# A hand-written order for the first seven slots of an attention and expert block

## The chip, the cores and the metric

The kernel runs on one core of a Trainium2 chip. Time is the device time of one execution in microseconds (us). The median of 3 runs before the change is 843.74 us (842.83 to 845.68). The core has five engines that run side by side, each taking its own instructions strictly in the order of the program: TensorE (PE in the profile, with PEld for its weight loads), VectorE (DVE), ScalarE (ACT), GpSimd (POOL) and SyncE (SP), which here only issues transfers. They wait for each other with semaphores.

## The reference, cut to what matters

Eight sequences of 256 tokens with 256 features go through an attention layer with a layer norm before and after it, and then through a layer of eight experts and a shared expert. All is float32. Only the beginning of the attention is touched by the change.

```python
x = x + _layernorm(_L0_attn_ref(_layernorm(x), w_qkv, w_o, qn_g, qn_b, kn_g, kn_b))
x = x + _layernorm(_L0_ffn_ref(_layernorm(x), ...))
...
qkv = jnp.einsum('bsh,oh->bso', x, w_qkv)          # 16 heads of q, 4 of k, 4 of v, 128 wide
q = _layernorm(q, qn_g, qn_b)                      # per head, over its 128 features
k = _layernorm(k, kn_g, kn_b)
q = q * cos + _rotate_half(q) * sin                # the same for k
scores = jnp.einsum('bhqd,bhkd->bhqk', q, k) / jnp.sqrt(jnp.float32(D))   # causal
weights = jax.nn.softmax(scores, axis=-1)
attn = jnp.einsum('bhqk,bhkd->bhqd', weights, v)
return jnp.einsum('bsd,od->bso', attn, w_o)
```

## The kernel before

**Tiling.** A sequence is two tiles of 128 tokens. The weights w_qkv are six groups of 512 columns: groups 0 to 3 are q's heads, 4 is k and 5 is v. A *projection* is one group times one token tile, 128 x 512 (`multiply`, L366), so a sequence has twelve, taken in the order of groups 4, 5, 0, 1, 2, 3 with both tiles of each. They are numbered j = 0 to 11.

**The work on one projection.** The mean of each head's weights is taken off the weights themselves once (`centre`, L229 to L231), so that q and k come out with mean zero. Then `square` (ACT, L384), `deviation` (DVE sum of the squares, L390), `power` (POOL, to the power -1/2, L399), `normalise` (ACT, four pieces of 128, L408), `rope_cos` (DVE, L422), `rope_sin` (POOL, two halves, L434), `rope_offset` (POOL, L447), `rope_sum` (DVE, L455) and `turn_heads` (four transposes on PE, L470, and a copy on ACT, L471). A projection of v is only copied (ACT, L381). The gains and biases of the norm are folded into tables with the cosine and sine (`tables`, L213 to L222): `cg`, `sg` and `bb` for q and for k; q's are also scaled by the root of 1/128.

**The attention** of a sequence is twelve units (four groups; tile 0 with four heads, tile 1 with twice two heads): `score` (PE), `maximum` (DVE), `exponential` (ACT), `inverse` (DVE), `weights` (POOL or ACT), transposes (PE, L544), `copy_weights` (DVE, L549), `value` (PE, L562). Then come 32 output products per sequence (L581).

**The order** is written by hand: inside `tc.manual_schedule()` each engine gets its instructions in the order of the text. A loop over slots s issues, in slot s, the stages of projection s, the normalisation and rope of projection s - 1, the sum and turning of s - 2, and the unit s - 7 of the attention with its later stages behind it; outputs begin at slot 19. A slot number is a running number over sequences: twelve slots belong to each. The next sequence's x is prepared by `begins` at places 2 to 7 of the current one (`prepare`, `prepared`, `turn_x`). Before the loop come the first x and the centring of group 4; `tables("k")` is in slot 0, `tables("q")` in slot 3, and the centrings of groups 0 to 3 are in slots 1, 3, 5 and 7, all on DVE.

**Loads.** All are issued from SP in the order of the text: x of sequence 0, w of group 4, k's gain and bias (each copied from memory to all 128 partitions), cosine and sine, q's gain and bias, w of groups 5 and 0, x of sequence 1, the other w, the other x, then wo and the expert weights.

**PSUM**[...] two each for projections (`ps_mm`), transposes (`ps_tr`) and scores (`ps_sc`), one for values (`ps_av`) and one for outputs (`ps_o`).

## Time and profile before

| | |
|---|---|
| median of 3 runs | 843.74 us |
| the profiled execution | 841.31 us |
| its span | 839.6 us |
| mean granted TensorE clock | 0.974 |
| busy PE, PEld | 751.9 us (90%), 552.4 us (66%) |
| busy DVE, ACT, POOL | 551.9 us (66%), 434.1 us (52%), 487.6 us (58%) |

The page cuts the span into 40 equal slices and gives each engine's busy share in tenths (9 is 90% or more), and the TensorE clock that was granted, in tenths of full speed. A line of instructions reads: source line, engine, operation, output<-inputs, shape. "A <- B" among the waits says that A stood idle until B was done. The chain is followed back from the last instruction, at each step to what released it. Durations of PE are those of pipelined instructions: one may be reported with 592 ns and the next begin 430 ns after it.

### The profile page before, as it was taken

Reading aid. Unit: us, or ns where it says so; the run is one execution under the profiler, and the core shown is the slowest. Engines: PE = TensorE matmul, PEld = TensorE weight load, DVE = VectorE, ACT = ScalarE, POOL = GpSimd, SP = SyncE. Lnnn points to the kernel's source line nnn. Section 1 sums busy time; section 2 is a strip of 40 time slices with the busy share of each in tenths; the row PEclk is TensorE's granted clock in tenths of the full one; section 3 lists DMA queues with packets and bytes.
Section 4 is the critical chain, followed back from the end, with each engine's and each line's share of the span. In section 5 each row is a group of like instructions: output and inputs, shape, how many; then the busy total and the mean of one; then the engine's idle time right before and its main releaser. Section 6 shows DMA issues by size and latency. Waiting matters only on the chain.

```text
span 839.6 us, 11874 instructions
## 1 busy us (share of the span) xinstructions
PE 751.9 (90%) x3770; PEld 552.4 (66%) x3770; DVE 551.9 (66%) x1392; ACT 434.1 (52%) x1393; POOL 487.6 (58%) x523
## 2 busy tenths in 40 slices
PE   4478999999999999999999999998988999998881
PEld 1246667767676676767667676776767867775561
DVE  4587676778778778877877887577653443234565
ACT  1247776657556675665667566576522323332230
POOL 3387587667748766784876678487111052236653
PEclk9699999999999999999999999999999999999997
DMA  8500000000000000000000000004002022224452
GB/s 263 164 1 1 1 1 1 7 1 7 7 1 7 1 7 1 7 7 1 8 1 7 2 7 7 1 7 139 7 7 73 9 88 77 63 89 126 130 146 75
DMA packets 27485, 32.66 MB, mean 39 GB/s; under 512 B 3040, under 2 KB 23616, under 8 KB 27424
## 3 DMA queue, kind: packets, MB, share of 16 engines
q1 hardware_dynamic: 24016, 22.59, 8.6%
q0 software_dynamic: 3408, 9.31, 4.1%
q8 instruction: 31, 0.51, 0.2%
q14 instruction: 30, 0.25, 0.1%
HBM read 22.59 MB, written 9.31 MB: 38 GB/s over the span
## 4 chain that ended last, share of the span: by engine, by line
PE 57%; POOL 16%; DVE 13%; ACT 8%; issue 5%; DMA 1%; POOLq 0%; SPq 0%; DVEq 0%; ACTq 0%
PE qkv L366 11%; PE o L581 8%; PE sc L482 6%; PE av L562 5%; PE gu L968 5%; ACT qn L408 5%; POOL rstds L399 5%; POOL t L434 5%; PE py L993 4%; POOL t L447 3%; PE tp L544 3%; PE tq L470 2%; PE g L270 2%; PE u L270 2%; PE sd L286 2%
## 5 line engine op out<-in xcount | busy, mean ns | idle before, releaser
L366 PE MATMUL qkv<-w_qkv,xnT 128*128 128x512 f32 x384 | 186.0, 609 | 8.3 <-DVE w_qkv L231 3.2
L408 ACT ACTIVATE qn<-qkv,rstds 128x128 f32<-128x128 f32 x320 | 91.5, 369 | 161.1 <-POOL rstds L399 161.1
L399 POOL TENSOR_TENSOR rstds<-ves,nhalf 128x4 f32<-128x4 f32 x80 | 87.1, 1088 | 115.1 <-DVE ves L390 115.1
L434 POOL TENSOR_TENSOR t<-qn,sg_q 128x256 f32<-128x256 f32 x128 | 122.1, 973 | 50.7 <-ACT qn L408 50.7
L581 PE MATMUL o<-wo_sb,oT 128*128 128x256 f32 x512 | 128.0, 389 | 0.0
L482 PE MATMUL sc<-kT,q 128*128 128x128 f32 x768 | 110.5, 279 | 1.8 <-ACT q L471 1.8
L513 ACT ACTIVATE ex<-sc,nmx 128x128 f32<-128x128 f32 (+1 forms) x256 | 107.7, 453 | 2.7 <-DVE nmx L502 2.4
L562 PE MATMUL av<-pT,v 128*128 128x256 f32 (+1 forms) x320 | 101.4, 432 | 7.3 <-ACT oT L573 6.6
L366 PEld LDWEIGHTS qkv<-w_qkv,xnT 128*128 128x128 f32 x384 | 67.9, 197 | 60.0 <-issue 49.5
L482 PEld LDWEIGHTS sc<-kT,q 128*128 128x128 f32 x768 | 102.4, 194 | 4.9 <-ACT q L471 2.9
L581 PEld LDWEIGHTS o<-wo_sb,oT 128*128 128x128 f32 x512 | 92.4, 193 | 9.5
L455 DVE TENSOR_TENSOR t<-t,t 128x512 f32<-128x512 f32 x80 | 55.3, 692 | 51.5 <-POOL t L447 51.5
L470 PEld LDWEIGHTS tq<-ident,t 128*128 128x128 f32 x320 | 38.1, 141 | 71.1 <-issue 51.5
L447 POOL TENSOR_TENSOR t<-t,bb_q 128x512 f32<-128x512 f32 x64 | 81.8, 1277 | 3.0
L549 DVE COPY pT<-tp 128x512 f32<-128x512 f32 x96 | 65.5, 682 | 18.2 <-PE tp L544 18.1
L533 ACT ACTIVATE ex<-ex,rr 128x256 f32<-128x256 f32 x128 | 59.5, 526 | 28.6 <-DVE rr L521 28.6
L562 PEld LDWEIGHTS av<-pT,v 128*128 128x128 f32 x320 | 59.1, 192 | 19.7 <-ACT oT L573 9.7
L470 PE MATMUL tq<-ident,t 128*128 128x128 f32 x320 | 49.3, 277 | 23.4 <-DVE t L455 23.3
L941 POOL DMA_INDIRECT xb<-xf_rows,src x39 | 38.5, 988 | 52.5 <-PE xt L951 37.7
L390 DVE TENSOR_REDUCE ves<-sq 128x4 f32<-128x516 f32 x80 | 54.8, 685 | 21.4 <-ACT sq L384 21.2
L544 PEld LDWEIGHTS tp<-ident,ex 128*128 128x128 f32 x384 | 47.7, 142 | 30.2 <-ACT q L471 9.6
L502 DVE TENSOR_REDUCE nmx<-sc 128x2 f32<-128x512 f32 (+1 forms) x96 | 64.2, 668 | 4.0 <-PE sc L482 3.4
(180 smaller groups left out, 1306.5 us busy)
## 6 DMA issues: line engine op xcount, KB each, us to landing
ys<-yb SPq DMA_DIRECT2D x39, 128.0 KB
w_qkv<-in_wqkvT SPq DMA_DIRECT2D x6, 512.0 KB
x_all<-in_x SPq DMA_DIRECT2D x8, 256.0 KB
wo_sb<-in_woT SPq DMA_DIRECT2D x1, 2048.0 KB
xf_rows<-xf SPq DMA_DIRECT2D x16, 128.0 KB
out<-yo SPq DMA_DIRECT2D x16, 128.0 KB
wgu_sb<-in_wg SPq DMA_DIRECT2D x2, 704.0 KB
wgu_sb<-in_wu SPq DMA_DIRECT2D x2, 704.0 KB
```

Source lines behind the costliest of these rows:

```text
L366: nc.tensor.matmul(ps.rearrange("p h d -> p (h d)"), lhsT=seqs[b]["xnT"][t][:, c, :], rhs=w_qkv[g][:, c, :], start=(c == 0), stop=(c == KC ...
L399: nc.gpsimd.tensor_tensor(rstd, now.pop(("ve", b, j)), nhalf, ALU.pow)
L408: nc.scalar.activation(qn[:, h, :], ps[:, h, :], AF.Copy, scale=rstd[:, h : h + 1])
L434: nc.gpsimd.tensor_tensor(t2[:, :, lo : lo + HD], qn[:, :, hi : hi + HD], sg[s][:, t : t + 1, lo : lo + HD].to_broadcast([P, REP, HD]), AL ...
L447: nc.gpsimd.tensor_tensor(t2, t2, bb[s][:, t : t + 1, :].to_broadcast([P, REP, D]), ALU.add)
L470: nc.tensor.transpose(tr[:, h, :], t1[:, h, :], ident)
L482: nc.tensor.matmul(sc[:, h, k * P : (k + 1) * P], lhsT=seqs[b]["qT"][g][:, r0 + h, t * P : (t + 1) * P], rhs=seqs[b]["kT"][:, g, k * P : ( ...
L513: nc.scalar.activation(ex[:, h, :], sc[:, h, :], AF.Exp, bias=nm[:, h : h + 1], accum_out=rs[:, h : h + 1],)
L544: nc.tensor.transpose(tr[:, c, :], ex[:, h, k * P : (k + 1) * P], ident)
L549: nc.vector.tensor_copy(pT, now.pop(("tp", b, u)).rearrange("p c q -> p (c q)"))
L562: nc.tensor.matmul(now["av"][:, r0 : r0 + nh, :].rearrange("p h q -> p (h q)"), lhsT=seqs[b]["v"][:, k, g * D : (g + 1) * D], rhs=pT[:, k ...
L581: nc.tensor.matmul(now["o", b, t], lhsT=seqs[b]["oT"][h // REP, t][:, h % REP, :], rhs=wo_sb[:, h, :], start=(h == 0), stop=(h == H - 1),)
```

## The change

Nothing is changed in what is computed. The loop now begins at slot 7; what slots 0 to 6 did is written out as a list. In it:

- 24 transposes of the identity come first on PE; their result is not read.
- The first sequence's projections are taken as v tile 0, k tile 0, k tile 1, v tile 1, then q as before. Projections 0, 3, 4 and 5 write to banks of scores, values and outputs.
- The offset is added to the cosine product on DVE (`rope_offset_early`) for projections 1, 2, 4, 5 and 6, in place of POOL's `rope_offset`.
- `centre` is split: `means` finds the negative mean on DVE; group 4 is centred on DVE, and groups 0 to 3 on ACT in eight pieces each (`centre_on_act`). Those of groups 2 and 3 are in slots 7 and 9.
- Gains and biases are loaded as four rows in one partition and multiplied by a row of ones on PE, which lays them on all 128 partitions; ACT copies the product to SBUF. q's rows are scaled before that, in place of q's tables. k's tables are made on POOL and q's on DVE.
- ACT issues the loads of these rows and of cosine and sine; SP issues x of sequence 0, w of groups 4, 5, 0, then x of sequence 1 and the rest.
- x of sequence 1 is prepared in slots 7 to 10 in place of slots 2 to 7; that of the other sequences is prepared where it was.

In the diff, the renaming of `projections[j]` to `projections[b][j]` is left out.

```diff
     load_x(0)
-    w_qkv = {4: load_w(4)}
+    w_qkv = {g: load_w(g) for g in groups[:3]}
...
-    gb = {}
-    for s, ga, ba in (("k", kn_g, kn_b), ("q", qn_g, qn_b)):
-        for n, a in (("g", ga), ("b", ba)):
-            gb[s, n] = sh.tile([P, 1, D], F32, tag=f"{n}_{s}", name=f"{n}_{s}", bufs=1)
-            nc.sync.dma_start(out=gb[s, n][:, 0, :], in_=a.partition_broadcast(P))
-        if s == "k":
-            nc.sync.dma_start(out=cos_sb, in_=cos.rearrange("(t p) d -> p t d", p=P))
-            nc.sync.dma_start(out=sin_sb, in_=ssin.rearrange("(t p) d -> p t d", p=P))
+    gb_all = sh.tile([P, 4, D], F32, tag="gb", name="gb_all", bufs=1)
+    gb_row = gb_all[0:1]
+    for n, a in enumerate((kn_g, kn_b, qn_g, qn_b)):
+        nc.scalar.dma_start(out=gb_row[:, n, :], in_=a[None, :])
+    nc.scalar.dma_start(out=cos_sb, in_=cos.rearrange("(t p) d -> p t d", p=P))
+    nc.scalar.dma_start(out=sin_sb, in_=ssin.rearrange("(t p) d -> p t d", p=P))
...
+    ones_row = scratch[0:1, 2 * NT, :]
+    nc.gpsimd.memset(ones_row, 1.0)
...
-    def tables(s):
+    def tables(s, engine):
...
-        if s == "q":
-            for tab in (cg[s], sg[s], bb[s]):
-                nc.vector.tensor_scalar_mul(tab, tab, scale)
-
-    def centre(g):
+    def means(g):
         heads = w_qkv[g].rearrange("p c (h d) -> p (c h) d", d=D)
         wm = small.tile([P, KC * REP], F32, tag="wm", name=f"wm_{g}")
         nc.vector.tensor_reduce(out=wm, in_=heads, axis=AX.X, op=ALU.add)
-        nc.vector.tensor_scalar_mul(wm, wm, 1.0 / D)
+        nc.vector.tensor_scalar_mul(wm, wm, -1.0 / D)
+        return heads, wm
...
+    def centre_on_act(heads, wm):
+        for i in range(KC * REP):
+            nc.scalar.activation(
+                heads[:, i, :], heads[:, i, :], AF.Identity, bias=wm[:, i : i + 1]
+            )
...
+        projections = [[(5, 0), (4, 0), (4, 1), (5, 1)] + rest[4:]] + [rest] * (B - 1)
...
+            spare = {0: (ps_sc, "sc"), 3: (ps_sc, "sc"), 4: (ps_av, "av"), 5: (ps_o, "o")}
+            pool, tag = spare.get(b * NS + j, (ps_mm, "mm"))
+            ps = pool.tile([P, REP, D], F32, tag=tag, name=f"qkv_{b}_{j}")
...
+        def rope_offset_early(b, j):
...
+            nc.vector.tensor_add(t1, t1, bb[s][:, t : t + 1, :].to_broadcast([P, REP, D]))
...
         with tc.manual_schedule():
+            warm = ps_tr.tile([P, 4, P], F32, tag="tr", name="warm")
+            for k in range(WARM):
+                nc.tensor.transpose(warm[:, k % 4, :], ident, ident)
             for t in range(NT):
                 prepare(0, t)
+            for t in range(NT):
                 prepared(0, t)
+            found[4] = means(4)
             for t in range(NT):
                 turn_x(0, t)
+            centre(*found.pop(4))
+            multiply(0, 0)
+            nc.vector.tensor_scalar_mul(gb_row[:, 2:], gb_row[:, 2:], scale)
+            gbp = ps_o.tile([P, 4, D], F32, tag="o", name="gbp")
+            nc.tensor.matmul(
+                gbp.rearrange("p n d -> p (n d)"), lhsT=ones_row,
+                rhs=gb_row.rearrange("p n d -> p (n d)"), start=True, stop=True,
+            )
+            nc.scalar.copy(gb_all, gbp)
+            found[0] = means(0)
+            tables("k", nc.gpsimd)
+            tables("q", nc.vector)
+            centre_on_act(*found.pop(0))
+            multiply(0, 1)
+            square(0, 0)
+            square(0, 1)
+            multiply(0, 4)
             nc.vector.tensor_copy(identb, ident)
-            centre(4)
-            for s in range(B * NS + OUT + 5):
...
+            deviation(0, 1)
+            power(0, 1)
+            found[1] = means(1)
+            square(0, 4)
+            multiply(0, 2)
+            multiply(0, 5)
+            normalise(0, 1)
+            deviation(0, 4)
+            power(0, 4)
+            rope_cos(0, 1)
+            rope_offset_early(0, 1)
+            rope_sin(0, 1)
+            normalise(0, 4)
+            square(0, 2)
+            rope_cos(0, 4)
+            rope_offset_early(0, 4)
+            rope_sin(0, 4)
+            deviation(0, 2)
+            power(0, 2)
+            centre_on_act(*found.pop(1))
+            rope_sum(0, 1)
+            turn_heads(0, 1)
+            rope_sum(0, 4)
+            turn_heads(0, 4)
+            multiply(0, 3)
+            multiply(0, 6)
+            normalise(0, 2)
+            square(0, 3)
+            square(0, 5)
+            rope_cos(0, 2)
+            rope_offset_early(0, 2)
+            rope_sin(0, 2)
+            deviation(0, 5)
+            power(0, 5)
+            found[2] = means(2)
+            normalise(0, 5)
+            square(0, 6)
+            rope_sum(0, 2)
+            turn_heads(0, 2)
+            rope_cos(0, 5)
+            rope_offset_early(0, 5)
+            rope_sin(0, 5)
+            deviation(0, 6)
+            power(0, 6)
+            for s in range(FIRST, B * NS + OUT + 5):
```

## The prediction

> **What bounds the kernel now.** I read the page's slices first, then busy time by stretch, then the waits and the chain of the first 60 us, then the timeline there.
>
> ```profile
> PE   4478999999999999999999999998988999998881
> DVE  4587676778778778877877887577653443234565
> POOL 3387587667748766784876678487111052236653
> PEclk9699999999999999999999999999999999999997
> ```
>
> A slice is 21 us. PE is full from the sixth slice to near the end; in the first two it is under half busy, and the second has granted clock 0.6. The stretches, in columns PE, PEld, DVE, ACT, POOL, granted clock, DMA share, GB/s:
>
> ```profile
> 11.00:53.00 42.00, 24.32 (x55) 11.08 (x55) 25.52 (x49) 10.32 (x28) 18.79 (x19) 0.80 0.52 171
> 53.00:117.00 64.00, 55.87 (x277) 36.96 (x276) 45.26 (x80) 44.32 (x148) 46.36 (x46) 0.97 0.00 1
> 117.00:600.00 483.00, 467.21 (x2477) 345.33 (x2476) 364.69 (x880) 308.10 (x1019) 333.33 (x339) 1.00 0.03 10
> ```
>
> Slots 0 to 6 lie in 11 to 53 us and no engine is more than 61% busy there: this stage is bound by waiting. The waits of the first 60 us (us in total, times, longest) say for whom:
>
> ```profile
> POOL rstds L399 <- DVE ves L390: 21.4, 2, 11.9
> ACT qn L408 <- POOL rstds L399: 17.3, 6, 4.6
> PEld tq L470 <- DVE t L455: 14.2, 3, 8.1
> ```
>
> and the chain (start, us, what) says why:
>
> ```profile
> 26.61 1.34 DVE xn L251
> 27.96 0.33 DVE cg_q L213
> ...
> 30.50 1.14 DVE wm L229
> 31.66 0.18 DVE wm L230
> 31.87 1.23 DVE w_qkv L231
> 33.09 0.61 DVE t L455
> 33.71 0.04 issue
> 33.75 1.12 PE tq L470 x4
> 34.87 3.43 PE qkv L366 x4
> ```
>
> VectorE works strictly in order. The sum of k's second tile (L455) stands behind q's tables and a centring; PE, with nothing to do meanwhile, falls to half clock and takes 3.43 us for four matmul pieces that take 1.73 later. From 53 to 117 us (slots 7 to 18) the chain alternates between POOL and ACT's normalisation, about 5.5 us a slot: L399 1.0, L408 1.15, L434 1.92, L447 1.26. From slot 19 PE carries the chain. Everything after slot 7 follows its predecessor, so time saved before slot 7 moves the end by as much, unless slots 7 to 10 return it.
>
> **How I cost the start.** I put the new order of instructions into the four engines' queues: each starts at the later of its engine's freedom and its inputs, with spacings from rows (VectorE 128x512 tensor op 0.61, reduction 0.60, weight-mean reduction 1.13 plus 0.17; POOL power 1.0; ACT normalisation 4 x 0.29; square or copy 0.48; projection 1.73 at full clock, 3.43 at half). One thing more is needed, seen in the timeline:
>
> ```profile
> 18.61 0.69 DVE L422 TENSOR_TENSOR t<-qn,cg_k 128x512 f32<-128x512 f32 x1 [2.31 <-ACT qn L408]
> 26.55 1.26 POOL L447 TENSOR_TENSOR t<-t,bb_k 128x512 f32<-128x512 f32 x1
> 26.61 1.34 DVE L251 TENSOR_SCALAR xn<-x_all,mv_x,rstd_x 128x256 f32<-128x256 f32 x1 [1.08 <-POOL rstd_x L246]
> ```
>
> The xn scaling takes 0.41 at its fastest, and 1.34 when it starts just behind a POOL tensor op, ending 0.14 after it: whichever has begun, the other waits. Reductions and POOL's power are not caught in this (L390 keeps 0.69 beside POOL). The same walk over the old order puts the normalisation of slot 7 (projection 6) at 51.7 us and that of projection 10 at 73.7; the trace has 52.52 and 74.27. It is 0.6 to 0.8 short, which I carry over.
>
> **The new start, in order.** (1) x lands at 3.6, as before; both tiles are normalised by 6.1. (2) The mean of group 4's weights, 1.21 + 0.18, now precedes the two 0.42 copies of the turned x: 7.8. In the old order the first projection waited until 11.37 for the centring, since it was k; now it is v, which needs none. (3) That projection, 7.8 to 9.7; the product with ones, two pieces of 0.43, to 10.5; ACT's copy 0.6, to 11.15. (4) q's tables on VectorE, seven ops, 1.9 us (27.96 to 29.89 in the old chain); k's on POOL beside them. POOL's 256-element op takes 0.73 (the residual add) and its 512-element one 1.26, so 0.46 for 128: 3 x 0.66 + 4 x 0.40 as spacings, 3.6. Under the exclusion they run one after the other: 11.15 + 1.9 + 3.6 = 16.7. (5) Power of k's first tile to 17.7; normalisation to 18.8. (6) Then VectorE's run of cosine, offset, cosine, offset, 18.9 to 21.4, keeps POOL's sines out until 21.3; sines of projections 1 and 4 to 24.6; power of 2 to 25.6; its normalisation behind two head copies to 27.7; sines to 30.3; power of 5, normalisation to 32.4; sines 33.7 to 35.1; power of 6 to 36.0. Slot 7's normalisation starts at 36.1. (7) PE idles from 18.8 to 24.0. The trace's clock fell to 0.5 about 25 to 38 us, around such a gap, so I let projection 3, and what follows to 28 us, run at half: v's copy is late on ACT, with the next square behind it; 1.5 us. Slot 7 at 37.6, with 0.6 carried over 38.2, against 52.5: **14.3 us won.**
>
> **What slots 7 to 10 return.** Centring of groups 2 and 3 goes to ACT, 8 x 0.29 = 2.3 us each, ahead of the exponentials in slots 7 and 9; the next normalisation queues behind. ACT idled 1.74 and 0.94 us before those. The second sequence's x moves to slots 7 to 10: two power ops of 0.55 on POOL, two scalings and copies of 0.4 on VectorE; slot 7's offset (1.26) leaves POOL. The walk has 23.3 us from projection 6's normalisation to that of 10, against 22.0 in the old order: **1.3 to 1.5 us back.** At 0.37 per ACT piece, its reported length, slot 9 loses 1.4 more.
>
> **Edits that I cost at nothing.** The six loads moved to ACT's queue: about 0.45 us of issue each (2.7 us) in ACT's idle first 10 us; without that cover they would delay the copy of step 3. SP then has x, w4, w5, w0 in a row. With the tables beside them, 1.57 MB must land by 7.8 us for step 3: from 2.0 us at 300 GB/s 7.2 us; at the 228 of the first active microsecond 8.9, which costs 1.2. The four 64 KB broadcasts go; the 15 to 59 GB/s of 6 to 8 us goes with them, but no engine waited there. Ones by memset, 0.1 on POOL before its first power. Spare PSUM banks: v's copies free both score banks before the first score at about 32, the output bank is free after the 11.15 copy, the value bank long before slot 9. VectorE loses four centrings of 1.14 and gains five adds of 0.61. ACT's biased Identity is in no row. A table load is 1.28 (ACT_TABLE_LOAD, L384), so 0 to 2.6; [...]I take 0.
>
> **The 24 transposes[...].** They run from the identity's completion at 1.8 us; transposes at half clock are some 0.22 apart, so they end by 7.1, before x can be turned. The row: projections starting at 11.37 ran 0.86 apart until 14.8 and 0.43 apart after, so 3.4 us of PE work ended half clock; by the row the first projection finds full clock at 7.8. [...] Then the first projection takes 3.4, the product 1.7 and the turned x comes 0.4 later: 3.0 us less won. No stretch of this trace is transposes alone. I take the row, narrowly: here they would be dense[...].
>
> **Sum.** 841.3 (profiled execution: span 839.6 plus 1.7 around it) - 14.3 + 1.5 = 828.5. The median of the runs shown, 843.7, is 2.4 above the profiled one: 831.0, likely own range 828.5 to 833.
>
> **Rivals.** (a) The transposes leave the clock at half: 831.0 + 3.0 = 834.0; the row is silent[...]. (b) PE stays warm across the 5 us gap and POOL slips its sines between VectorE's ops: 1.5 back, and up to 2.4 from the waits of step 6: about 827.5; against it, clock 0.5 in the old gap. (c) Most is returned: ACT becomes the bound in slots 7 and 9. With 0.5 us per centring piece it returns 3.7 more, with late w5 1.2 more: 836. The SBUF-to-SBUF scaling of 256 (L533, 0.41 apart) speaks against 0.5 for 128. (d) Slower: PE at half clock in the stage where PE sets the pace, after slot 19. A slot of 5.75 us then costs 5.75 more; 2.2 such slots cancel the 12.8; four give 831 + 23 = 854. Clock rows of 1.00 from 80 to 500 us speak against it.
>
> **Chances.** As walked 0.45, (a) 0.30, (b) 0.12, (c) 0.09, (d) 0.04. 0.3% is 2.5 us, about what a measurement tells: the first three are all faster, of (c) some 0.03 within; faster 0.93, same 0.03, slower 0.04. From 825.5 to 837 nearly all of the first three and half of (c) is held, with room for a walk that is 2 us off either way.
>
> **What would show it.** Right: first projection at about 8 us and its pieces 0.43 apart; tables done near 16.7, DVE's first; slot 7's normalisation at 37 to 39; projection 10's 13 us before 74.3; the same 5.75 us per slot afterwards. Wrong: pieces 0.86 apart at 8 us (a); no PE gap near 20 us (b); POOL or ACT waiting in slots 7 to 9 for the centring of ACT (c); clock under 1 after 120 us (d); a table load between the copy and the centring; the first projection waiting for a DMA.

## The result, and the profile after

The changed kernel takes 830.44 us (median of 4 runs, 828.14 to 832.62) against 843.29 us for the kernel before in the same comparison (4 runs, 841.73 to 845.68). The ratio is 0.9845, with an interval of 0.9808 to 0.9882. The gain is 12.85 us. Forecast were 831.0 us and a gain of 12.8.

The profiled execution has a span of 829.3 us. Its slices are below (40 of them, 20.7 us each, busy share in tenths, and the granted TensorE clock).

```profile
PE   7588899999999999999999999997979999998681
DVE  7776667687878778787877876687544452244465
POOL 5678578386757748675774868486111142246653
PEclk9899999999999999999999999999999999999896
```

PE, which was at 4 and 4 tenths in its first two slices, is now at 7 and 5. The dip of the clock to 6 in the second slice is a dip to 8. From the fourth slice on the rows look much as before. The busy time by stretch, in columns PE, PEld, DVE, ACT, POOL (each with its count), granted clock, DMA share and GB/s:

```profile
8.00:38.00 30.00, 21.08 (x58) 9.90 (x59) 23.88 (x36) 15.07 (x43) 18.72 (x20) 0.89 0.69 227
38.00:103.00 65.00, 53.65 (x264) 34.60 (x266) 44.45 (x85) 48.23 (x162) 46.76 (x48) 0.99 0.00 1
103.00:590.00 487.00, 469.72 (x2474) 348.23 (x2499) 367.97 (x892) 310.46 (x1027) 333.97 (x340) 1.00 0.03 10
```

The first row answers to 11 to 53 us of before. The start has shrunk from 42 us to 30, and VectorE, at 80%, is now the busiest engine of it. In the second stretch ACT has more to do (48.23 us instead of 44.32), with the centrings of two groups now there. The third is the same work at the same pace. The waits of the first 60 us (us in total, times, longest) that answer to those of before:

```profile
ACT qn L423 <- POOL rstds L414: 10.9, 5, 3.0
...
PE tq L493 <- DVE t L478: 9.5, 3, 6.1
...
POOL rstds L414 <- DVE ves L405: 2.6, 3, 0.9
```

POOL's wait (for the sum of the squares) fell from 21.4 us to 2.6: VectorE no longer stands with other work between a square and its power. One wait of 6.1 us for the rope's sum is left. It is the new gap of PE. The timeline of the start (start, us, engine, line, what, in brackets the idle time before it and what ended it):

```profile
8.49 1.95 PE L381 MATMUL qkv<-w_qkv,xnT 128*128 128x512 f32 x4 [1.49 <-DVE xnT L371]
...
10.38 1.12 PE L776 MATMUL gbp<-gb_all,scratch 1*128 1x512 f32 x2
...
11.54 0.59 ACT L780 COPY gb_all<-gbp 128x512 f32<-128x512 f32 x1 [5.05 <-PE gbp L776]
...
15.96 0.79 POOL L223 TENSOR_TENSOR bb_k<-bb_k,so_k 128x256 f32<-128x256 f32 x1
16.09 0.75 DVE L789 CAST identb<-ident 128x128 bf16<-128x128 f32 x1
16.76 0.68 DVE L405 TENSOR_REDUCE ves<-sq 128x4 f32<-128x516 f32 x1
...
17.52 1.03 POOL L414 TENSOR_TENSOR rstds<-ves,nhalf 128x4 f32<-128x4 f32 x1 [0.76 <-DVE ves L405]
...
25.20 1.97 PE L493 MATMUL tq<-ident,t 128*128 128x128 f32 x8 [6.12 <-DVE t L478]
...
26.96 5.04 PE L381 MATMUL qkv<-w_qkv,xnT 128*128 128x512 f32 x8
...
36.88 0.69 DVE L478 TENSOR_TENSOR t<-t,t 128x512 f32<-128x512 f32 x1
36.94 1.50 POOL L414 TENSOR_TENSOR rstds<-ves,nhalf 128x4 f32<-128x4 f32 x1
...
38.47 1.14 ACT L423 ACTIVATE qn<-qkv,rstds 128x128 f32<-128x128 f32 x4 [3.01 <-POOL rstds L414]
```

The last line is the normalisation of slot 7, my anchor. It stood at 52.52 us before and stands at 38.47 now: 14.05 us won. The normalisation of projection 10 went from 74.27 to 61.72, so slots 7 to 10 gave back 1.5 and 12.55 are left. The sum over experts that opens the expert stage (`total`, L837 before and L940 after) moved from 664.1 to 651.3, 12.8 earlier. (On the way there the lead was smaller for a while. The part on the prediction has the reason.) The spans differ by only 10.3, because the expert stage of this profiled execution is 2.5 us longer than in the one of before (178.0 us from there to the end against 175.5) with the same instructions. From 767.5 to 787.5 us its clock is 0.83, and ACT waits 5.1 us there once. In the profiles of the twelve experiments below, on other chips, this stretch takes 166.3 to 168.8 us with the same instructions, so I count the difference as scatter of that stage and not as an effect of the change. The medians, 12.85 apart, agree with the 12.8 that arrived at its opening.

### The profile page after: what moved, and what is told of

Same layout as the page of the kernel before. It is cut to its first block, busy times and chain, and to the rows that moved or that the text cites. A ratio compares the mean times of both kernels' runs of the same rounds, so it can differ in the third digit from the quotient of the medians.

```text
span 829.3 us, 11934 instructions
## 1 busy us (share of the span) xinstructions
PE 751.9 (91%) x3765; PEld 555.8 (67%) x3796; DVE 549.6 (66%) x1384; ACT 443.8 (54%) x1426; POOL 488.7 (59%) x526
## 4 chain that ended last, share of the span: by engine, by line
PE 57%; POOL 15%; DVE 13%; ACT 10%; issue 5%; DMA 1%; another core or an unknown queue 1%; POOLq 0%; SPq 0%; DVEq 0%; ACTq 0%
PE qkv L381 11%; PE o L604 7%; PE sc L505 6%; PE gu L1071 6%; ACT qn L423 5%; POOL rstds L414 5%; PE av L585 5%; POOL t L449 4%; PE py L1096 4%; PE tp L567 3%; POOL t L462 3%; PE tq L493 3%; PE g L280 2%; PE u L280 2%; PE sd L296 2%
## 5 line engine op out<-in xcount | busy, mean ns | idle before, releaser
L381 PE MATMUL qkv<-w_qkv,xnT 128*128 128x512 f32 x384 | 183.2, 600 | 1.6 <-DVE xnT L371 1.5
L462 POOL TENSOR_TENSOR t<-t,bb_q 128x512 f32<-128x512 f32 x61 | 77.6, 1272 | 2.8
L437 DVE TENSOR_TENSOR t<-qn,cg_q 128x512 f32<-128x512 f32 x64 | 47.7, 746 | 26.2 <-ACT qn L423 26.2
```

Of the source, the lines that this page charges most:

```text
L381: nc.tensor.matmul(ps.rearrange("p h d -> p (h d)"), lhsT=seqs[b]["xnT"][t][:, c, :], rhs=w_qkv[g][:, c, :], start=(c == 0), stop=(c == KC ...
L462: nc.gpsimd.tensor_tensor(t2, t2, bb[s][:, t : t + 1, :].to_broadcast([P, REP, D]), ALU.add)
```

## The experiments

Four groups of runs were made on four other chips, where the kernel before takes about 832 us instead of 843. So each ratio is against the kernel before on the same chip, and the effects are read from the same two anchors: the normalisation of slot 7 (38.47 in the profile after) and that of projection 10 (61.72). In an exact repetition of the changed kernel on another chip (the fifth experiment) the first anchor is 38.97, so a shift of half a microsecond in one profile is not yet an effect. Where a shift arises is read from the instructions between.

### 1. The 24 transposes left out

This kernel leaves out the 24 transposes of the identity, whose result nobody reads.

```diff
-            warm = ps_tr.tile([P, 4, P], F32, tag="tr", name="warm")
-            for k in range(WARM):
-                nc.tensor.transpose(warm[:, k % 4, :], ident, ident)
```

> The 24 transposes of the identity at the start are left out; nothing else. If they end the half clock, as I took it, the first projection's pieces run 0.86 us apart instead of 0.43, the product with ones is late by 1.7 us and more, and the normalisation of slot 7 starts about 2.6 us later than the 38.47 of the changed kernel: 40.5 to 41.5; the median rises by about 2.6. If transposes don't count for the clock, the changed kernel's first projection had full clock for another reason, and nothing moves by more than 0.4.

Measured: ratio 0.9871 (0.9833 to 0.9908), slot 7 at 40.17, projection 10 at 63.40: 1.7 us later, where 2.6 were expected. The timeline, and the busy time in the stretch from 8 to 12 us:

```profile
8.24 3.64 PE L380 MATMUL qkv<-w_qkv,xnT 128*128 128x512 f32 x4 [1.01 <-DVE xnT L370]
...
11.81 1.12 PE L772 MATMUL gbp<-gb_all,scratch 1*128 1x512 f32 x2
```

```profile
8.00:12.00 4.00, 3.76 (x5) 1.37 (x6) 3.19 (x6) 0.00 (x0) 0.00 (x0) 1.00 1.05 390
```

The four pieces take 3.64 us here and 1.95 with the transposes in front. So transposes alone did end the half clock here, as the row of the trace had suggested. The product with ones takes 1.12 in both kernels: behind the slow projection the clock is full here too. The projection takes 1.7 longer but begins 0.25 earlier, so that 1.4 arrive at the power of k's first tile (18.94 instead of 17.52). The other 0.3 come behind PE's gap, where the half clock ends at 32.1 us instead of 29.9.

The granted clock in the last row reads 1.00 while the pieces run at half speed. It does so in the kernel before too:

```profile
11.00:14.60 3.60, 3.23 (x4) 1.51 (x5) 2.21 (x8) 0.00 (x0) 0.00 (x0) 1.00 1.06 397
```

There the four pieces from 11.37 on take 3.60 us, and the first change of the clock that the trace records, to full, is at 14.60. In the profile after the first one is at 5.97, ahead of the projection, whose pieces take 1.95. So at the start the spacing of the pieces is the measure, not this column.

### 2. k's tables on VectorE too

```diff
-            tables("k", nc.gpsimd)
+            tables("k", nc.vector)
```

> k's tables are made on VectorE, ahead of q's, instead of on POOL. If the two engines exclude each other on these ops, as I took it, the fourteen ops took the sum of both (about 4.6 us) in the changed kernel, and on VectorE alone they take about 3.9 and the following copy of the identity is no longer held: the power of k's first tile starts 0.9 to 1.2 us earlier (16.3 to 16.6 instead of 17.52) and slot 7's normalisation 1.0 to 1.6 earlier (36.9 to 37.5). Rival, without exclusion: POOL's share was free, VectorE's 3.9 us come one after the other and end later than its 1.9: the power starts no earlier and slot 7 is the same or up to 1 us later.

Measured: ratio 0.9839 (0.9798 to 0.9881), power of k's first tile at 16.88 instead of 17.52, slot 7 at 36.99, 1.5 us earlier. VectorE alone makes both sets in 3.9 us, the two engines side by side in 4.6. In the profile after, VectorE's table ops of 256 elements take 0.95 beside POOL and 0.42 alone, and the cast of the identity behind them 0.75 and 0.22. The expected 16.3 to 16.6 for the power was not quite reached.

Only 0.64 of the 1.5 are the tables'. The chain from that power to the turning of the heads (24.56 instead of 25.20) is 0.64 earlier throughout. The other 0.84 come behind it, with the clock. The first row is of the profile after, the others are of this experiment:

```profile
23.04:29.87 6.83, 4.67 (x12) 3.11 (x13) 3.67 (x6) 3.61 (x11) 3.83 (x4) 0.50 0.65 201
...
24.09:27.50 3.41, 2.94 (x10) 2.42 (x11) 1.02 (x2) 1.52 (x4) 1.28 (x1) 0.50 0.96 301
27.50:30.90 3.40, 3.01 (x7) 0.96 (x6) 2.64 (x4) 1.78 (x5) 2.53 (x3) 1.00 0.03 11
```

Half clock lasts 6.83 us there and 3.41 here, so the eight pieces behind the turning take 4.19 instead of 5.04. The copy of v that waits for the first four is 1.50 earlier (28.83 instead of 30.33). So the 1.5 is one profile's sum of a better split and a shorter half clock.

### 3. The PE gap filled with 48 transposes

```diff
             multiply(0, 5)
+            again = ps_tr.tile([P, 4, P], F32, tag="tr", name="again")
+            for k in range(AGAIN):
+                nc.tensor.transpose(again[:, k % 4, :], ident, ident)
             normalise(0, 1)
```

AGAIN is 48.

> 48 more transposes of the identity are put on PE in the gap ahead of the first turning of heads (19 to 25 us). If the gap costs the clock, as step 7 has it, the eight pieces of projections 3 and 6 take 3.5 us instead of 5.04 and slot 7's normalisation starts about 1.5 us earlier (36.7 to 37.3). Rival: the later pieces were not on the path (v's copy hides behind the normalisation), and slot 7 moves by less than 0.4; or the transposes themselves delay the heads, and it moves later.

Measured: ratio 0.9816 (0.9778 to 0.9854), slot 7 at 37.05, 1.4 us earlier. The stretch 24 to 31 us in the profile after, and then the stretches of the filled gap and behind it in this experiment, in the columns of the first table by stretch:

```profile
24.00:31.00 7.00, 5.80 (x15) 3.51 (x16) 3.54 (x5) 3.32 (x10) 4.00 (x4) 0.58 0.48 152
```

```profile
19.00:25.00 6.00, 5.37 (x49) 5.13 (x47) 5.39 (x7) 4.73 (x17) 5.41 (x6) 1.00 1.12 345
25.00:32.00 7.00, 4.72 (x16) 2.25 (x16) 4.46 (x8) 3.46 (x9) 4.46 (x4) 1.00 0.34 107
```

With the gap empty, the clock behind it is 0.58 and the eight pieces of projections 3 and 6 take 5.04 us. With the gap full of transposes it stays 1.00 and the pieces take 3.60. That the difference is 1.4 too is chance, since not all of these pieces are on the path. v's copy comes 2.0 earlier (28.35 instead of 30.33) and leaves the path. The next power then waits for the other branch, through the head copy, the normalisation and the rope, so that 1.42 are left at that power (30.80 instead of 32.22) and at the anchor. The step "PE idles and then runs at half, 1.5 us" is shown with its cause.

### 4. The early offset back on POOL

```diff
-            rope_offset_early(0, 1)
             rope_sin(0, 1)
+            rope_offset(0, 1)
```

The same edit is made for projections 4, 2 and 5.

> In the list of the first seven slots the offsets of projections 1, 4, 2 and 5 go back to POOL, behind each one's sines; that of projection 6 stays on VectorE. If POOL is what the stage waits for, four ops of 1.26 us replace four of 0.61 that each kept POOL out for as long: slot 7's normalisation comes about 2 us later (40 to 41). Rival: the adds on VectorE keep POOL out for as much as they take off it, and nothing moves by more than 0.5.

Measured: ratio 0.9874 (0.9836 to 0.9912), slot 7 at 40.39, 1.9 us later. VectorE's offset of 1.1 us, which runs while POOL makes the sines, replaces one of 1.26 to 1.59 behind them on POOL.

### 5. The changed kernel again

It has no edit. It ran with experiments 6 to 8 on one chip.

> The changed kernel once more, beside the other kernels of this group. Its start should be fixed by the order of the queues: slot 7's normalisation at 38.5 and projection 10's at 61.7, within 0.3. The part of the execution behind the attention took 2.2 us longer in the profiled execution of the changed kernel than in that of the kernel before, with the same instructions; if that is scatter of the gathers there and not an effect of the change, its length differs here again, and the ratio to the kernel before is again 0.981 to 0.988.

Measured: 820.77 us against 831.99, ratio 0.9868 (0.9849 to 0.9886), slot 7 at 38.97, projection 10 at 62.20. The gain is 11.2 us on this chip. Both anchors are 0.5 later than in the profile after, where at most 0.3 was expected: 0.2 from the start of the first projection on, the rest behind PE's gap, where the half clock ends at 30.9 instead of 29.9. The chain begins here with a transfer:

```profile
1.79 6.79 DMA w_qkv<-in_wqkvT
```

The first projection waits here for the weights of group 5, not for VectorE.

### 6. Experiments 2 and 3 together

```diff
-            tables("k", nc.gpsimd)
+            tables("k", nc.vector)
...
             multiply(0, 5)
+            again = ps_tr.tile([P, 4, P], F32, tag="tr", name="again")
+            for k in range(AGAIN):
+                nc.tensor.transpose(again[:, k % 4, :], ident, ident)
```

> Both edits that helped: k's tables on VectorE ahead of q's, and 48 more transposes in PE's gap at 19 to 25 us. If the two act on different parts of the path (tables before 18 us, clock after 25 us), the gains of 1.48 and 1.42 add up to 2.4 to 2.9: slot 7's normalisation at 35.6 to 36.1 instead of 38.47. Rival: both shorten the same wait, and it stays at about 37.0.

Measured: 816.42 us on the chip of experiment 5, ratio 0.9813 (0.9797 to 0.9829), slot 7 at 36.35, projection 10 at 59.58. This is the best version. It beats the kernel before and, with intervals that don't overlap, the changed one (820.77 us). At the anchor the two edits bring 2.6 us against experiment 5 and 2.1 against the profile after, from which their 2.9 one by one were read; 35.6 to 36.1 was expected. The missing 0.8 is about what experiment 2 had from the clock (0.84): filling the gap takes this half clock away (the granted clock is 1.00 from 25 to 32 us; from 32 to 38 it is 0.72), so the 0.8 was counted twice. The medians differ by 4.35. In the two profiled executions the spans differ by 4.9, of which 2.5 are there when the expert stage opens (647.3 against 649.8) and 2.4 come in that stage, with the same instructions. What the edits are shown to bring is the 2.5. Experiment 3 alone has nearly the same ratio, so that the tables add to it is seen at the anchor only (36.35 against 37.05, about the 0.64 of experiment 2).

### 7. Groups 2 and 3 centred on VectorE

```diff
-                    centre_on_act(*found.pop(centre_at[s]))
+                    centre(*found.pop(centre_at[s]))
```

> The centrings of groups 2 and 3 in slots 7 and 9 are done on VectorE in one op each, where they were before the change, instead of in eight pieces on ACT; their means are found where the changed kernel finds them. If ACT's 2.3 us ahead of the exponentials are what slots 7 to 10 return, the time from slot 7's normalisation (38.5) to that of projection 10 falls from 23.25 to 22.3 to 22.8 us. Rival: VectorE takes the same time back (1.14 us each, and held by POOL's ops), and it stays at 23.2 or rises.

Measured: ratio 0.9863 (0.9846 to 0.9881), slot 7 at 38.42 and projection 10 at 62.69. The interval between the anchors is 24.27 us, against 23.25 with the centring on ACT and 21.75 before the change. So the rival came true: between these anchors VectorE is the worse place for both centrings. That does not clear ACT's centring, since it is not the old order either. Before the change the centrings of groups 0 to 3 stood at the head of slots 3, 5, 7 and 9 (31.87, 41.00, 51.57 and 62.51 us), not in slots 1, 3, 5 and 7 as written above. Group 2's was thus ahead of the first anchor, and only group 3's lay between the two. Now both do. The timeline of slot 7 shows what VectorE's place costs:

```profile
42.67 1.22 DVE L235 TENSOR_TENSOR w_qkv<-w_qkv,wm 128x1024 f32<-128x1024 f32 x1
42.84 1.93 POOL L414 TENSOR_TENSOR rstds<-ves,nhalf 128x4 f32<-128x4 f32 x1
```

POOL's power, 1.02 us otherwise, takes 1.93 because it starts just behind VectorE's centring. In slot 9 it takes 2.00 behind a centring that takes 2.13.

### 8. In the kernel before, q's tables two slots earlier

```diff
-        tables_at = {0: "k", 3: "q"}
+        tables_at = {0: "k", 1: "q"}
...
+                if s == 1:
+                    centre(0)
-                if s + 1 < NS and projections[s + 1][1] == 0 and projections[s + 1][0] < 4:
+                if s + 1 < NS and projections[s + 1][1] == 0 and projections[s + 1][0] in (1, 2, 3):
```

> The kernel before, with q's tables and the centring of group 0 moved from slot 3 to slot 1, where VectorE waits; nothing else. If the stall of 27 to 34 us came from VectorE's order, as I read the chain, the first projection of q starts 3 to 4 us earlier and slot 7's normalisation at 48.5 to 49.5 instead of 52.52; the time falls by 3 to 4. Rival: the stall is of POOL's chain or of PE's clock, and the start moves by less than 1.

Measured: 828.73 us against 831.99, ratio 0.9952 (0.9928 to 0.9975), slot 7 at 49.58 instead of 52.52, 2.9 us earlier, and 2.9 at projection 10. The stall that my first view named, k's second sum standing behind q's tables and a centring, is real and costs 3 us. A move of two calls in the old kernel takes it out. It is about a fifth of the whole gain at slot 7, not most of it.

### 9. The centrings put where ACT waits

```diff
-        means_at = {8: 3}
-        centre_at = {7: 2, 9: 3}
+        means_at = {7: 3}
+        centre_at = {8: 3}
...
             turn_heads(0, 2)
+            centre_on_act(*found.pop(2))
...
-                if s in centre_at:
-                    centre_on_act(*found.pop(centre_at[s]))
                 each(power, j)
...
                 each(exponential, u)
+                if s in centre_at:
+                    centre_on_act(*found.pop(centre_at[s]))
```

> The centrings of groups 2 and 3 stay on ACT but move into two holes of 3.0 us that its queue shows in the changed kernel: group 2's behind the head copy of projection 2, before slot 7's normalisation; group 3's behind the exponentials of slot 8, its means to slot 7. If ACT's pieces ahead of the exponentials are what slots 7 to 10 return, the time from slot 7's normalisation to that of projection 10 falls from 23.25 to 21.9 to 22.4 us. Rival: the x of the second sequence and POOL's ops in slots 7 and 8 return it, and it stays above 22.8.

Measured: ratio 0.9864 (0.9826 to 0.9902), slot 7 at 40.58, projection 10 at 64.00, interval 23.42. The return stays. Slots 7, 9 and 10 go back to 5.5 us each, but slot 8 takes 6.94. Its rows on POOL and VectorE:

```profile
44.84 1.21 DVE L230 TENSOR_REDUCE wm<-w_qkv 128x8 f32<-128x1024 f32 x1
...
47.09 0.17 DVE L544 RECIPROCAL rr<-rs 128x4 f32<-128x4 f32 x1
...
47.34 1.04 POOL L551 TENSOR_TENSOR ex<-ex,rr 128x512 f32<-128x512 f32 x1 [1.31 <-DVE rr L544]
...
48.34 1.86 POOL L449 TENSOR_TENSOR t<-qn,sg_q 128x256 f32<-128x256 f32 x2
```

The means of group 3, moved into slot 7 with the centring, take 1.21 us of VectorE ahead of the reciprocals. POOL waits 1.31 for these with its weights, and its sines queue behind them. This execution also started two microseconds later at slot 7. Its first projection took 3.64 us, at half clock, although the 24 transposes were there (see the last section).

### 10. Experiments 2, 3 and 9 together

```diff
-            tables("k", nc.gpsimd)
+            tables("k", nc.vector)
...
+                nc.tensor.transpose(again[:, k % 4, :], ident, ident)
...
+            centre_on_act(*found.pop(2))
...
-        means_at = {8: 3}
-        centre_at = {7: 2, 9: 3}
+        means_at = {7: 3}
+        centre_at = {8: 3}
```

> k's tables on VectorE, 48 more transposes in PE's gap, and the centrings in ACT's holes, together. If the three act on different waits, slot 7's normalisation starts at 36.0 to 36.6 and that of projection 10 at 58.0 to 58.9, against 61.7 of the changed kernel and 59.6 with the first two alone; the time is 1 us below that of the first two: a ratio to the kernel before of 0.978 to 0.982.

Measured: 819.82 us against 832.21, ratio 0.9851 (0.9822 to 0.9880), slot 7 at 38.31, projection 10 at 61.73. The interval, 23.42, is that of experiment 9. The start lost 2 us to a first projection at half clock again (3.56 us, begun at 8.78 after 1.88 of waiting for the weights of group 5). It is no improvement on experiment 6.

### 11. The old loads under the new order

SP loads as before the change: x, group 4, the broadcasts of gains and biases with cosine and sine between them, then groups 5 and 0. The product with ones and its copy are left out.

```diff
-    w_qkv = {g: load_w(g) for g in groups[:3]}
+    w_qkv = {4: load_w(4)}
...
-        nc.scalar.dma_start(out=gb_row[:, n, :], in_=a[None, :])
-    nc.scalar.dma_start(out=cos_sb, in_=cos.rearrange("(t p) d -> p t d", p=P))
-    nc.scalar.dma_start(out=sin_sb, in_=ssin.rearrange("(t p) d -> p t d", p=P))
+        nc.sync.dma_start(out=gb_all[:, n, :], in_=a.partition_broadcast(P))
+        if n == 1:
+            nc.sync.dma_start(out=cos_sb, in_=cos.rearrange("(t p) d -> p t d", p=P))
+            nc.sync.dma_start(out=sin_sb, in_=ssin.rearrange("(t p) d -> p t d", p=P))
...
```

> The changed kernel with the loads of the kernel before: all from SP in the old order, gains and biases copied to all partitions by the transfers themselves; the row of ones, the product with it and ACT's copy are left out. If the old order's 1.3 MB ahead of group 5 are late, the first projection waits to about 11.4 us (8.5 in the changed kernel), group 0's means to about 12.8 (10.15) and slot 7's normalisation comes 2 to 2.5 us later: 40.5 to 41. Rival: the product and the copy, which stood on the path, cost as much as the broadcasts, and slot 7 moves by less than 0.5.

Measured: ratio 0.9885 (0.985 to 0.992), slot 7 at 41.49, 3.0 us later, more than expected. The timeline shows who waited:

```profile
13.23 3.60 PE L380 MATMUL qkv<-w_qkv,xnT 128*128 128x512 f32 x4 [5.87 <-DMA w_qkv<-in_wqkvT]
14.51 1.22 DVE L229 TENSOR_REDUCE wm<-w_qkv 128x8 f32<-128x1024 f32 x1 [2.33 <-DMA w_qkv<-in_wqkvT]
...
15.97 2.45 ACT L241 ACTIVATE w_qkv<-w_qkv,wm 128x128 f32<-128x128 f32 x8
...
19.41 0.69 DVE L404 TENSOR_REDUCE ves<-sq 128x4 f32<-128x516 f32 x1 [1.41 <-ACT sq L398]
```

The weights of group 5 come 4.7 us later and those of group 0 some 4.4. The chain goes through group 0: its mean, its centring on ACT, and behind that in ACT's queue v's copy and k's square, for which VectorE waits. Beside this the first projection runs at half clock after its wait (3.60 us for four pieces). k's tables, made without the product, were done at 11.3, before k was even projected, which helped nothing. So the loads are worth 3 us in this order: 2.7 at the power of k's first tile, the rest behind PE's gap. How much of that belongs to the order in SP's queue, how much to the four broadcasts and how much to the lost clock, was not separated.

### 12. Closing the last PE gap of the start

This is experiment 6 with the loads of cosine and sine behind group 5 on SP, and six transposes after the turning of x. The diff is against experiment 6.

```diff
-    w_qkv = {g: load_w(g) for g in groups[:3]}
+    w_qkv = {g: load_w(g) for g in groups[:2]}
...
-    nc.scalar.dma_start(out=cos_sb, in_=cos.rearrange("(t p) d -> p t d", p=P))
-    nc.scalar.dma_start(out=sin_sb, in_=ssin.rearrange("(t p) d -> p t d", p=P))
+    nc.sync.dma_start(out=cos_sb, in_=cos.rearrange("(t p) d -> p t d", p=P))
+    nc.sync.dma_start(out=sin_sb, in_=ssin.rearrange("(t p) d -> p t d", p=P))
+    w_qkv[0] = load_w(0)
...
                 turn_x(0, t)
+            bridge = ps_tr.tile([P, 4, P], F32, tag="tr", name="bridge")
+            for k in range(6):
+                nc.tensor.transpose(bridge[:, k % 4, :], ident, ident)
```

> k's tables on VectorE and 48 transposes in PE's gap, as in the kernel with both edits, and two more: cosine and sine are issued by SP behind group 5's weights instead of by ACT beside them, and 6 transposes of the identity follow the turned x on PE. In all profiled executions the first projection waited 0.8 to 1.9 us for group 5's weights, and in two of nine it then ran at half clock, which cost 2 us. If cosine and sine on the other queue delay these weights, the first projection starts at 8.2 to 8.4, with no wait for a transfer; if idle PE ahead of it loses the clock, its pieces are 0.43 apart again. Slot 7's normalisation at 35.8 to 36.4, median at or up to 2 us below the kernel with both edits, ratio to the kernel before 0.978 to 0.982. Rival: group 5's weights are late for another reason (the first projection still waits), or cosine and sine are now late for the tables, and slot 7 stays at 36.4 or later.

Measured: 818.45 us against 831.61, ratio 0.9836 (0.9806 to 0.9865), slot 7 at 36.66, projection 10 at 59.89: no earlier than experiment 6. Slot 7 and the projection miss the times expected, and the rival (36.4 or later) fits.

```profile
8.10 0.87 PE L775 MATMUL bridge<-ident 128*128 128x128 f32 x6 [1.16 <-DVE xnT L373]
...
8.81 1.88 PE L383 MATMUL qkv<-w_qkv,xnT 128*128 128x512 f32 x4
```

The bridge begins at 8.10 us only, since its PSUM buffer comes free with VectorE's copy of the turned x, so it closes little of the gap that it was meant for. The projection begins at 8.81, directly behind it, so the row can't say when group 5's weights had landed. It ran at full clock, as in experiment 6 without a bridge.

## Why the prediction was right, and where its steps were not

**The frame held, with some luck.** Time won before slot 7 did move the end, less what slots 7 to 10 return: 14.05 less 1.5 was seen, 14.3 less 1.5 was forecast. But it did not stay one for one all the way. The lead of the normalisations over those of before is 12.9 us at 103 us and 11.3 from 133 us on, and 12.8 again where the expert stage opens. Each of the two profiled executions has a stretch at half clock where PE sets the pace, the changed one at 101.6 us, the old one at 591.5:

```profile
101.55:104.96 3.41, 3.19 (x13) 2.93 (x14) 1.81 (x5) 2.22 (x10) 2.16 (x3) 0.50 0.00 0
...
591.47:594.88 3.41, 3.41 (x10) 2.59 (x9) 1.29 (x5) 2.44 (x11) 0.56 (x1) 0.50 0.11 38
```

The first cost 1.6 us, the second 1.7, and they cancel. So in a single profile the lead behind slot 10 is known to within 1.7 us only. From 105 to 590 us the clock is 1.00, so rival (d) did not occur but for this one stretch, and (a) fell with experiment 1. Of (c) nothing came beyond the 1.5 that were forecast. One table load was seen on ACT, 1.28 us at 5.21 while ACT waited for its loads, and none between the copy and the centring. That there would be none, as the walk took it, no row of before had shown.

**Steps (2) and (3) were about 1 us too early.** The first projection was put at 7.8 and began at 8.49, and the copy of the product ended at 12.13 instead of 11.15. x was normalised at 6.37 instead of 6.1 and its first turned tile copied at about 8.0 (7.62 and half of 0.75). That is 0.2 of the 0.7. The rest is the landing of group 5's weights, which I had worked out as 7.2 to 8.9 and taken at the early end (the late end is 1.1 us later, where the prediction wrote 1.2). In the eleven profiles of this start with the new loads, the first projection begins at 8.16 to 8.81. Five of the rows name this transfer. Five name the copy of x. In experiment 1 that fits (copied at 8.14, projection at 8.24). In the other four the first tile's copy had been over for some 0.4 us, and that the weights were late there too is inferred from it. In experiment 12 the bridge stands between. So the expectation of experiment 12, that all had waited for these weights, said more than the rows show.

**Step (4) ended at the right time by two errors.** The tables were walked as VectorE's first and POOL's after, 5.5 us. Seen were 4.6 us, both engines taking turns op by op (VectorE's last table op ends at 16.17, POOL's at 16.75). That made up for the late copy. Then the cast of the identity (L789, 0.75), which the text of the program puts ahead of k's sum and I had left out of the walk, put the power at 17.52 to 18.55 instead of ending at 17.7. Giving everything to VectorE, experiment 2, is 0.64 us better at that power: the exclusion makes the split a loss.

**Step (6) came out right by two errors too.** POOL's sines of projections 1 and 4 ended at 24.53 (walked: 24.6). But they were not kept out until VectorE's run was over. The first began at 20.42, inside that run, which lasted to 23.95 instead of 21.4. The two engines took turns, as one half of rival (b) had it, and needed 4.7 us from 19.82 on where 5.7 from 18.9 on were walked. That took back the 0.9 by which k's first power was late.

**Step (7) held, mechanism and size.** The gap of PE was 6.1 us, and the chain behind it goes through the four pieces at half clock, v's copy and the square behind it, as forecast. (In the kernel before the clock was granted at 0.50 from 24.84 to 38.49 us, so it fell ahead of the gap there, which lasts from 27.21 to 33.75, and not in it.) It cost 1.42, as experiment 3 shows, where 1.5 was put. The other half of (b), a PE that stays warm, did not come. Slot 7 was due at 38.2 and came at 38.47. With errors of up to a microsecond on the way that offset each other, 0.3 is better than the walk is.

**The transposes.** The choice of the row was right: 24 of them open the clock here (four pieces in 1.95 us, against 3.64 without), and 48 hold it for 5.4 us (granted clock 1.00 from 19 to 25 us). Rival (a) stood on no row of the trace of before, and its 0.30 was an estimate of mine. The term for losing it was larger than what experiment 1 measured, 3.0 against 1.7. It had 1.7 for the projection, 0.85 for a product with ones at half speed, which took 1.12 us in experiment 1 as in the profile after, and 0.4 for an x that is turned later behind slow transposes, which leaving them out does not test.

**"No engine waited there".** So I wrote of the old broadcasts. It is true of the old order, in which v was needed late, and wrong as a price of the edit. Without the new loads the new order loses 3.0 us. For the broadcasts the walk had simply assumed the weights to be there. An order of work and the order of its loads have to be priced together.

**"POOL's power is not caught."** It is: 1.50 us at 36.94, beside VectorE's sum at 36.88, and 1.93 and 2.00 in experiment 7. The first of these lies directly ahead of the anchor and costs 0.5 us in the changed kernel. The 0.6 that was carried over without a cause is about as large, which is luck. In the kernel before no power up to 75 us takes more than 1.07, so that trace did not show it.

**The return in slots 7 to 10** has the predicted size, but only in part the predicted reason. The chain of the changed kernel goes through these slots as follows (start, us, what):

```profile
40.58 1.22 ACT w_qkv L242 x5
...
41.90 1.00 ACT w_qkv L242 x3
42.90 1.41 ACT ex L536 x8
...
44.33 0.19 DVE rr L544
...
44.59 0.79 POOL ex L551
...
45.59 1.86 POOL t L449 x2
47.45 0.51 POOL rstd_x L256
47.96 1.23 POOL t L462
49.19 0.99 POOL rstds L414
...
50.20 1.14 ACT qn L423 x4
```

The centring holds back the exponentials, these the reciprocals, these POOL's weights, and POOL's sines queue behind. Then 0.51 for x stands between the sines and the offset. Slots 7 to 10 take 5.68, 6.05, 6.00 and 5.52 us, where they took 5.43, 5.50, 5.32 and 5.50. So two centrings now lie in slots 7 to 10, where one lay before. When the centring is moved, another piece takes its place: POOL's held power in experiment 7, the means ahead of the reciprocals in experiment 9. In all nine profiles with the centring where the change puts it, the interval is 23.23 to 23.26, whatever happened earlier. x of sequence 1 is in these slots in every version of the changed kernel, so what it takes of the 1.5 us stays open. The chain shows 0.51 of it.

**What each part is worth.** Taken away one at a time from the changed kernel: the loads 3.0, the offsets on VectorE 1.9, the transposes 1.7. The placing of q's tables and group 0's centring, taken alone in the old kernel, is 2.9. These are 9.5 of the 14 us, but they are read from different kernels, and each of the first three holds some 0.3 us from where the half clock ends, so they need not add up. The rest, among it the early projections and the centring on ACT, was not taken apart.

## What to carry to other kernels

When one stage is bound by waiting, write the instructions of the new order into each engine's queue with measured spacings and read off when each starts; that gave a slot within 0.3 us of the trace here, with errors of up to 1 us on the way that offset each other. Only transfers that are walked in the same way are priced. A filler that keeps PE busy through a known gap is worth a trial when matmuls behind the gap are on the path: here 48 useless transposes bought 1.4 us. When an edit that has nothing to do with PE moves the end by more than it moves its own instructions, look where the clock changed: of 1.5 us in experiment 2, 0.84 were the clock's. Before work is split between VectorE and POOL, look whether their rows lengthen beside each other, since one engine alone can be faster than both, as with the tables here (3.9 us against 4.6).

## What the runs showed of the hardware that was not expected

- **Transposes opened the clock and held it.** With 24 of them ahead of a projection its four pieces take 1.95 us, without them 3.64 (experiment 1). With 48 of them in PE's gap the granted clock is 1.00 from 25 to 32 us (experiment 3), with the gap empty 0.58 from 24 to 31 (profile after).
- **Half clock around a gap of PE lasted longer in one profile than in another.** It lasted 6.83 us in the profile after, with PE busy for 4.67 of them, 3.41 in experiment 2, with PE busy for 2.94, and 13.65 in the kernel before (from 24.84 on), with PE busy for 7.11. What sets its beginning and its end was not shown.
- **A short warm-up can be lost.** In experiments 9 and 10 the first projection ran at half clock (3.64 and 3.56 us) after the same 24 transposes, and the granted clock from 8 to 12 us is 0.58 in both. The first two rows are of experiment 9, the last two of experiment 6, which kept the clock:

```profile
4.00:8.00 4.00, 2.76 (x18) 2.31 (x16) 3.37 (x11) 1.28 (x1) 1.27 (x2) 1.00 1.00 321
8.00:12.00 4.00, 3.37 (x4) 1.17 (x4) 3.16 (x6) 0.00 (x0) 0.00 (x0) 0.58 1.05 393
...
4.00:8.00 4.00, 2.82 (x18) 2.38 (x16) 3.38 (x11) 1.28 (x1) 1.27 (x2) 1.00 1.01 350
8.00:12.00 4.00, 3.58 (x8) 1.38 (x9) 3.07 (x6) 0.53 (x2) 0.00 (x0) 1.00 1.04 362
```

From 4 to 8 us PE was busy for 2.76 us in experiment 9 and for 2.82 in experiment 6. The last idle time before the projection was 1.62 us in experiment 9, 1.88 in experiment 10 and 1.50 in experiment 6. Idle time alone does not decide: 2.20 us of it before 34.21 us in the profile after cost nothing (four pieces in 1.88 us behind it). No run was made to test what does.

- **A tiny POOL operation was held by VectorE's sums and centrings.** The power of 128x4 elements takes 1.02 us, 1.38 (at 24.63) and 1.50 (at 36.94) beside 128x512 sums, and 1.93 to 2.00 beside a 128x1024 centring. Beside the scaling of x (0.41 at 42.88) it keeps its 1.02.
- **The granted clock reads 1.00 at the start** while matmul pieces run at half speed: from 11.00 to 14.60 us in the kernel before, where four pieces take 3.60, and from 8 to 12 in experiment 1, where they take 3.64.
